# Two transformer layers on one core: where gathers, first weight loads and one pairing copy stand in the order of work

## The chip, the core and the metric

The kernel runs on one core of a Trainium2 chip. Its time is device time in microseconds (us) for one execution. Before the change four runs gave 1397.26 to 1401.92 us, with a median of 1398.56. The engines are named as in the profile: PE is TensorE (matmuls; PEld is its weight load), DVE is VectorE, ACT is ScalarE, POOL is GpSimd. SP only issues DMAs. ACT and POOL issue DMAs too, POOL's being the gathers, whose row numbers come from a tile of indices.

## What is computed

The input x has 64 batches of 32 tokens of 256 numbers. Two layers are added to it, each an attention and a feed-forward part, and each with parameters that a batch picks by an index (`itok_*`). Cut to its core, in float32:

```python
x = x + attn0(einsum('bct,bcd->bdt', x, weights[itok_198]), ...)   # 16 heads of 128, 64 slots a head
x = x + ffn0(cond2(x, Wg, Wu, Wd, Ag, Bg, Au, Bu, Ad, Bd, itok_7)) # low-rank ways per batch
x = x + attn1(cond1(x, W, A, Bm, scalings, itok_6), ...)           # low-rank way per batch
x = x + ffn1(cond3(x, W, b, itok_15), w_gate_up, w_down)           # one of 16 matrices per batch

# in attn0
q, k = rope(hs @ Wq.T), rope(hs @ Wk.T)
s  = clip(hs @ Ws1.T @ Ws2.T + bs2)
ok = exp(-cumlogsumexp(s)) * (tril(q k^T) @ exp(s))
# in cond2, with A = Ag[itok], and so on
gate = x @ Wg + (x @ A) @ B
h = silu(gate) * up
y = h @ Wd + (h @ Ad[itok]) @ Bd[itok]
```

`ffn0` rounds its weights to three values, `ffn1` rounds weights and activations to 8-bit steps.

## The kernel before

The order of instructions is written by hand: each engine runs its own instructions in the order in which the program emits them, and waits for what they read and for the memory that they overwrite.

**Start.** SP loads indices, two tiles of x, wqp (the first 512 columns of Wq), the four strips of ws2 (17 rows each, line 727), more of x, and then the other weights. ACT's queue loads the constants and ws1c. wqp and wkp hold the columns as given; ACT copies them into the order that the rotation wants (L720, two copies each, into wq and wk). The loop over (wq, wk) requests one and copies it before it comes to the next, and wkp is requested by ACT itself (L717). Meanwhile POOL gathers 16 tiles cwt (L744), DVE spreads them into own (L756), TensorE makes hs of the first half group (L766), ACT copies it to hsT (L774), TensorE makes the low rank r (L783) and ACT moves it to rT (L787). Weight tiles of this part come from ten slots; a load into a slot waits until its last tile has been read.

**Phase one, turns -1 to 33.** Each turn works on several of 32 steps (a group of 4 heads by a quarter of two x tiles). For step n+1 it runs slots_exp (L892 reads ws2 and rT, four matmuls, the fourth reading the fourth strip), project_qk (L820; DVE multiplies, L831 and L832; POOL adds, L834 and L835) and cumsum; for step n scores (L940), attend, weigh (POOL makes qe, L987), project_v (L850), project_g (L867) and turn_qe (TensorE reads qe, L1006); for n-1 mix, values, gate and norm (POOL's power, L1077); for n-2 leave (L1100, added to x by DVE, L1106). The generator tabulate() is advanced once after each turn from the third. It writes tables for the later gathers into DRAM: alin and blin; then, for each of eight chunks in one advance, the own tables own_in and own_out by nine gathers into two staged tiles and three stores on SP; then alora and blora. The generator chunk_0() runs the first chunk's first half of phase two inside turns 31 to 33.

**Between the phases** the program emits fetch_down(0), a gather; fetch_linear(0), two loads on SP; lw; and the loads of the attention's weights wqk, sixteen small DMAs (L1231) of which ACT issues eight and SP eight.

**Phase two, turns 0 to 7 of turn2, then drain.** Each turn works on one chunk of 256 tokens: gate_up (L519) with its ways (gate_up_adapters: L534, Silu on ACT L541, product on DVE L542), pair_down (ACT copies the gathered ways of Ad from the tiles ag into adp, L547), down_adapters (TensorE reads adp, L560; DVE writes ud, L566), down (L576, L581; it reads cdt), ffn_up (L600, L604, L605), ffn_down (L619, L624), linear_adapters (L633) and linear (L651). Between them stand attention and scores of chunk n-1 and the experts and 8-bit layers of chunk n-2 (run_experts L1431, quant_up L1461, quant_h, turn_h L1485, quant_down L1501). The gathers for later use are fetch_in (8, into ag), fetch_out (4, into bx), fetch_down (1) and fetch (8 expert matrices `we` and 2 biases `eb`). In gather() a `held` gather first has DVE copy its column of indices into a small tile (L443, sixteen tiles in turn), so that POOL's gather (L445) cannot come before DVE has reached that place; one that is not held reads the index table directly.

Of the kernel before, what the change touches and what calls it, by code (L numbers as in the profile page):

```python
# [15 lines left out]
P = 128  # L16
B = 64
T = 32
D = 256
# [59 lines left out]
def mk_kernel(  # L79
# [250 lines left out]
    own_in = dram.tile([8 * P, D], F32, tag="own_in", name="own_in")  # L330
    own_out = dram.tile([8 * P, D], F32, tag="own_out", name="own_out")

    def tabulate():
        def ways_in(table, src, lo, rows):
            to = table.rearrange("(a p) v -> p a v", p=P)
            with nc.allow_non_contiguous_dma(reason="ranks of an adapter"):
                nc.sync.dma_start(
                    out=to[:, :, lo : lo + 16], in_=src[rows, :].rearrange("p (a i) -> p a i", i=16)
                )

        def every_other(k):
            return slice(k, D, 2)

        for k in range(2):
            ways_in(alin, laT, k * 16, every_other(k))
        yield

        def staged():
            return first.tile([P, D], F32, tag="sg", name="staged", bufs=2)

        t = staged()
        nc.sync.dma_start(out=t, in_=lb)
        nc.vector.tensor_scalar(t, t, scal, None, MULT)
        nc.sync.dma_start(out=blin, in_=t)
        yield
        for ch in range(8):
            rows = slice(ch * P, (ch + 1) * P)
            t = staged()
            for b in range(8):
                at = ch * 8 + b  # L360
                gather(t[:, b * 32 : (b + 1) * 32], alin, idx("lora2", it)[:, at : at + 1], False)
            for k in range(2):
                nc.sync.dma_start(
                    out=own_in[rows, :].rearrange("p (j k b i) -> p k j b i", j=4, k=2, b=2)[:, k],
                    in_=t.rearrange("p (j b k i) -> p k j b i", j=4, k=2, b=2)[:, k],
                )
            t = staged()
            gather(t, blin, lidx[:, ch : ch + 1], False)
            nc.sync.dma_start(out=own_out[rows, :], in_=t)
            yield  # L370
        for i, src in enumerate((ag, au)):
            for k in range(2):
                ways_in(alora, src, k * 32 + i * 16, every_other(k))
            yield
        for k in range(8):
            ways_in(alora, ad, 64 + k * 16, slice(k * P, (k + 1) * P))
            if k % 2:
                yield
        for half in range(2):
            for i, src in enumerate((bg, bu)):  # L380
                rows = slice((2 * half + i) * P, (2 * half + i + 1) * P)
                nc.sync.dma_start(
                    out=blora[rows, :].rearrange("p (k f) -> p k f", k=4),
                    in_=src.rearrange("p (k half f) -> p half k f", k=4, half=2)[:, half, :, :],
                )
                yield
# [283 lines left out]
    with ExitStack() as s1:  # L670
# [41 lines left out]
        ws1c = p1.tile([P, 2, 16], F32, tag="ws1c", name="ws1c")  # L712
        nc.scalar.dma_start(out=ws1c, in_=ws1T.rearrange("(c p) r -> p c r", p=P))

        for name, src, queue in (("wq", wqT, nc.sync), ("wk", wkT, nc.scalar)):
            t, to = slot(f"{name}p", [P, 2, 512]), slot(name, [P, 2, 512])
            queue.dma_start(out=t, in_=src[:, :512].rearrange("(c p) f -> p c f", p=P))  # L717
            weights.setdefault(0, []).append(to)
            for c in range(2):
                nc.scalar.copy(  # L720
                    to[:, c, :].rearrange("p (half h r) -> p half h r", half=2, h=4),
                    t[:, c, :].rearrange("p (h half r) -> p half h r", h=4, half=2),
                )

        ws2 = p1.tile([P, 1024], F32, tag="ws2", name="ws2")
        for i in range(4):
            nc.sync.dma_start(out=ws2[32 * i : 32 * i + 17, :], in_=ws2T)
# [4 lines left out]
        nc.sync.dma_start(out=gnwt, in_=gnw)  # L732
        load_weights(0, ("wo",))
        nc.sync.dma_start(out=scal, in_=lscal)
        load_weights(1)
        ws1 = p1.tile([P, 2, 4, 32], F32, tag="ws1", name="ws1")
        nc.vector.memset(ws1, 0.0)

# [57 lines left out]
        own_weights(1, 2)  # L796
        condition(0, (0,))
        low_rank(0, (0,))
        own_weights(2, 4)

        cosb = const("cos").unsqueeze(1).to_broadcast([P, 16, T])
# [310 lines left out]
        def turn(n):  # L1112

            def on(i, f, *a):
                if 0 <= i < len(steps):
                    f(i, *a)

            def more(*at):

                if n in at:  # L1120
                    next(beyond)

            def ahead():
                if 2 <= n < len(steps):
                    next(preparing, None)

            N = len(steps)
            on(n + 1, slots_exp)
            on(n, scores)
            more(N)  # L1130
            on(n - 1, mix)
            on(n + 1, slots_clip)
            more(N - 1)
            on(n - 2, leave)
            more(N - 1)
            on(n + 1, project_qk, "q", 0)
            on(n + 1, project_qk, "k", 0)
            if n == -1:
                condition(0, (1,))
                own_weights(4, 8)  # L1140
            if n < 2:
                condition(n + 2)
            on(n - 1, values)
            on(n, attend)
            on(n + 1, cumsum)
            more(N)
            on(n, weigh)
            on(n + 1, project_qk, "q", 1)
            on(n + 1, project_qk, "k", 1)
            on(n - 1, gate)  # L1150
            on(n, project_v)
            on(n, project_g)
            if n == -1:
                low_rank(0, (1,))
                own_weights(8, 16)
            if n < 2:
                low_rank(n + 2)
            if n == 1:
                small_tables()
                next(preparing)  # L1160
            ahead()
            more(N - 1)
            on(n, turn_qe)
            ahead()
            on(n - 1, norm)
            more(N)
# [16 lines left out]
            yield  # L1183

        beyond = chunk_0()
        tabulating = tabulate()
        for n in range(-1, len(steps) + 2):
            turn(n)
            if n in (25, 30, 31, 33):
# [26 lines left out]
    bdt = w.tile([P, D], F32, tag="bdt", name="bdt")  # L1216
    fetch_down(0, False)
    adp = w.tile([P, 4, 8, 2, 16], F32, tag="adp", name="adp")
    fetch_linear(0)
    ud = w.tile([P, 2, 4, T], F32, tag="ud", name="ud")  # L1220
    lw = load_w("lw", [P, 2, D], lwT.rearrange("(p c) f -> p c f", c=2))
# [182 lines left out]

    experts = {}

    def fetch(ch, b):


        got = experts.setdefault(ch, {})  # L1410
# [5 lines left out]
        else:  # L1416
# [1 line left out]
            if b == 8:  # L1418
                got[8] = work.tile([P, 2, D], F32, tag="eb", name="eb", bufs=1)
            to = got[8][:, b - 8, :]  # L1420
        gather(to, table, at, True)

    def run_experts(ch, groups=(0, 1)):
        c = chunks[ch]
# [89 lines left out]
    def turn2(n):  # L1514
# [20 lines left out]
        for k in range(8):  # L1535
            gu(k)
            if k == 3:
                if not begun:
                    on(n, gate_up_adapters, 0)
                on(n - 2, run_experts)  # L1540
                for i in range(4):
                    on(n - 1, attn_scores, i)
            elif k == 5:
                on(n - 1, attn_exp)
                on(n, pair_down)
            elif k == 6:
                on(n - 2, turn_y)
        if not begun:
# [2 lines left out]
        if n == 1:  # L1551
            project_values(0)
            tokens_in(2)
        on(n - 1, fetch, 0)
        on(n - 1, fetch, 1)
        on(n - 2, quant_up, 0)
        on(n - 2, quant_h, 0)
        on(n - 1, fetch, 2)
        on(n - 1, fetch, 3)
        on(n, down_adapters)  # L1560
        on(n + 1, fetch_in, 0)
        if not last:
            on(n - 2, quant_up, 1)
            on(n - 2, quant_h, 1)
        for b in range(1, 4):
            on(n + 1, fetch_in, b)
        on(n, down)
        on(n - 2, tokens_back)
        if n != 1:
            on(n + 1, tokens_in)  # L1570
        on(n + 1, fetch_in, 4)
        on(n - 1, fetch, 4)
        if not last:
            on(n - 2, turn_h, 0)
            on(n - 2, turn_h, 1)
        on(n - 1, attn_values)
        on(n, ffn_up, 0)
        on(n + 1, fetch_in, 5)
        on(n - 1, fetch, 5)
        on(n, ffn_up, 1)  # L1580
        on(n + 1, fetch_in, 6)
        on(n - 1, fetch, 6)
        on(n, ffn_up, 2)
        on(n + 1, fetch_in, 7)
        on(n - 1, fetch, 7)
        on(n, ffn_up, 3)
        on(n + 1, fetch_out, 0)
        on(n, ffn_up, 4)
        on(n + 1, fetch_out, 1)
        if last:  # L1590
            on(n - 1, attn_out)
        on(n, ffn_up, 5)
        on(n + 1, fetch_out, 2)
        on(n - 1, fetch, 8)
        on(n - 1, fetch, 9)
        if last:
            on(n - 2, quant_up, 1)
            on(n - 2, quant_h, 1)
            on(n - 1, run_experts)
            for b in range(8):  # L1600
                fetch(7, b)
        else:
            on(n - 2, quant_down, 0)
        on(n + 1, fetch_out, 3)
        on(n, ffn_down)
        if last:
            on(n - 2, turn_h, 0)
# [2 lines left out]
            on(n - 2, quant_down, 1)  # L1610
            on(n - 1, attn_out)
        on(n, linear_adapters)
        on(n + 1, fetch_down)
        on(n, linear)
        on(n + 1, fetch_linear)

    def drain():

        turn_y(6)
        queries_keys(7)  # L1620
        for b in range(8, 10):
            fetch(7, b)
        quant_up(6, 0)
        for k in range(4):
# [2 lines left out]
        project_values(7)  # L1627
        quant_down(5, 0)
        attn_weights(7)
        quant_up(6, 1)  # L1630
        attn_values(7, 2)
        quant_down(5, 1)
# [107 lines left out]
```

## Time and profile before

| | |
|---|---|
| median of the runs | 1398.56 us |
| the profiled execution | 1399.07 us, its span 1397.3 us |
| granted TensorE clock, mean | 0.999 |
| DVE, ACT, POOL busy | 65%, 36%, 39% |
| DMA | 70.27 MB, mean 50 GB/s |
| gathers `we`, mean of one on POOL | 948 ns, x64 |
| copy wk<-wkp on ACT | 1.14 us for two |
| copy adp<-ag on ACT | 1.14 us for two |
| L820 x8, the first / a later one | 3.62 / 1.99 us |
| a turn of phase one, L867 to L867, from 102.89 to 750.84 us | 22.96 to 23.84 us |

The profile is of one execution. Its page gives the busy time of each engine over the span; views of the trace give what an engine waited for (releaser, total, times, longest), the instructions in order of time (start, length, engine, line, tile written<-read), the DMAs issued in a stretch with the median time to landing, and the busy time in stretches.

### The profile page before, as it was taken

What the parts mean: (1) busy time and instruction counts of PE and PEld (TensorE: products, weight loads), DVE (VectorE), ACT (ScalarE), POOL (GpSimd) and SP (SyncE); (2) the same over time, 40 slices, a digit from 0 to 9 for tenths busy, and PEclk for the clock granted to TensorE, in tenths of its full rate; (3) what the DMA queues carried; (4) which work ended last, traced back from release to release, by engine and by line L of the source; (5) the groups of instructions that cost most, each with busy time, mean ns of one, the idle gap of its engine ahead of it and who ended that gap; (6) DMA issues with size and microseconds to landing.
All of it is one profiled execution on the core that took longest, in us unless ns stands there. A gap on an engine that the chain in (4) does not pass through costs nothing.

```text
span 1397.3 us, 37990 instructions
## 1 busy us (share of the span) xinstructions
PE 1363.9 (98%) x16332; PEld 1093.6 (78%) x16332; DVE 913.8 (65%) x1907; ACT 507.6 (36%) x1365; POOL 538.2 (39%) x601
## 2 busy tenths in 40 slices
PE   4999999999999999999999999999999999999997
PEld 3777777777777778777777788888787878888775
DVE  2687888887888888877777425463646364554665
ACT  2454545454545454545454213130312221222221
POOL 5332477777434333333444131423231405050220
PEclk9999999999999999999999999999999999999999
DMA  6120001311312000100001251312131304031220
GB/s 194 50 69 2 5 19 30 95 37 27 63 40 58 10 6 12 42 2 2 13 15 49 60 103 37 98 53 88 44 98 32 110 11 123 10 109 33 69 77 16
DMA packets 96864, 70.27 MB, mean 50 GB/s; under 512 B 66420, under 2 KB 83956, under 8 KB 96696
## 3 DMA queue, kind: packets, MB, share of 16 engines
q0 software_dynamic: 14848, 36.98, 9.2%
q1 hardware_dynamic: 73736, 25.37, 7.5%
q10 hardware_dynamic: 8112, 5.49, 1.4%
q8 instruction: 128, 2.10, 0.6%
q14 instruction: 40, 0.33, 0.1%
HBM read 63.49 MB, written 6.29 MB: 50 GB/s over the span
## 4 chain that ended last, share of the span: by engine, by line
PE 96%; DVE 1%; DMA 1%; ACT 1%; issue 1%; POOL 0%; ACTq 0%; SPq 0%; DVEq 0%
PE ps L820 16%; PE ps L1100 8%; PE ps L519 8%; PE ps L867 8%; PE ps L850 8%; PE ps L1461 6%; PE ps L600 5%; PE ps L576 4%; PE ps L1501 3%; PE ps L619 3%; PE ps L940 3%; PE ps L1049 2%; PE ps L534 2%; PE ps L1267 2%; PE ps L892 1%; PE ps L1067 1%
## 5 line engine op out<-in xcount | busy, mean ns | idle before, releaser
L445 POOL DMA_INDIRECT we<-in_ew,at x64 | 60.7, 948 | 287.0 <-DVE h L1468 213.5
L1106 DVE SCALAR_TENSOR_TENSOR x<-ps,f,x 128x256 f32<-128x256 f32 x256 | 120.7, 482 | 11.9 <-PE ps L1100 0.7
L820 PE MATMUL ps<-hsT,wq 128*128 128x256 f32 x512 | 126.2, 390 | 0.0
L820 PE MATMUL ps<-hsT,wk 128*128 128x256 f32 x512 | 120.9, 379 | 0.0
L1100 PE MATMUL ps<-wo,og 128*128 128x256 f32 x512 | 119.0, 385 | 1.3
L867 PEld LDWEIGHTS ps<-hsT,wg 128*128 128x128 f32 x512 | 97.3, 190 | 26.9 <-issue 15.1
L867 PE MATMUL ps<-hsT,wg 128*128 128x256 f32 x512 | 115.7, 379 | 0.0
L850 PE MATMUL ps<-wv,hsT 128*128 128x512 f32 x256 | 115.2, 593 | 0.0
L1056 ACT ACTIVATE sq<-ps 128x512 f32<-128x512 f32 x64 | 34.8, 595 | 213.0 <-PE ps L1049 213.0
L834 POOL TENSOR_TENSOR qT<-ra,rb 128x256 f32<-128x256 f32 x64 | 46.8, 731 | 168.8 <-DVE rb L832 168.7
L820 PEld LDWEIGHTS ps<-hsT,wq 128*128 128x128 f32 x512 | 95.5, 192 | 18.2 <-issue 4.8
L924 DVE RECIPROCAL enz<-ps 128x256 f32<-128x256 f32 x64 | 107.5, 1721 | 2.8 <-PE ps L915 2.8
L1100 PEld LDWEIGHTS ps<-wo,og 128*128 128x128 f32 x512 | 94.6, 190 | 17.0 <-DVE aT L947 5.2
L820 PEld LDWEIGHTS ps<-hsT,wk 128*128 128x128 f32 x512 | 97.4, 190 | 13.3
L1077 POOL TENSOR_TENSOR f<-f,mhalf 128x8 f32<-128x8 f32 x32 | 54.4, 1701 | 137.5 <-DVE f L1075 137.5
L978 ACT ACTIVATE qv<-ok,nmx 128x64 f32<-128x64 f32 x256 | 85.3, 334 | 30.8 <-DVE nmx L974 29.8
L831 DVE TENSOR_TENSOR ra<-ps,ct 128x512 f32<-128x512 f32 x128 | 85.9, 671 | 3.7 <-PE ps L820 2.0
L832 DVE TENSOR_TENSOR rb<-ps,ct 128x512 f32<-128x512 f32 x128 | 87.0, 680 | 0.0
L850 PEld LDWEIGHTS ps<-wv,hsT 128*128 128x128 f32 x256 | 48.6, 190 | 47.6 <-issue 45.9
L1461 PE MATMUL ps<-guT,y3T 128*128 128x352 f32 x256 | 79.8, 465 | 0.5 <-ACT y3T L407 0.5
L542 DVE TENSOR_TENSOR hT<-ps,sg 128x256 f32<-128x256 f32 x64 | 24.2, 420 | 83.8 <-ACT sg L541 83.8
L445 POOL DMA_INDIRECT ag<-alora,at x56 | 53.0, 947 | 55.6 <-DVE at L443 33.7
(235 smaller groups left out, 2818.0 us busy)
## 6 DMA issues: line engine op xcount, KB each, us to landing
x<-in_x SPq DMA_DIRECT2D x8, 256.0 KB, 16.5
wv<-in_wvT SPq DMA_DIRECT2D x4, 512.0 KB
wg<-in_wgT SPq DMA_DIRECT2D x4, 512.0 KB, 4.2
wo<-in_woT SPq DMA_DIRECT2D x4, 512.0 KB
wq<-in_wqT SPq DMA_DIRECT2D x12, 128.0 KB, 3.0
wk<-in_wkT SPq DMA_DIRECT2D x12, 128.0 KB, 4.2
row<-in_wgu ACTq DMA_DIRECT2D x11, 128.0 KB, 2.2
out<-res SPq DMA_DIRECT2D x5, 256.0 KB, 2.3
```

The lines of the kernel that those rows point to most:

```text
L445: nc.gpsimd.indirect_dma_start(out=to, out_offset=None, in_=table, in_offset=bass.IndirectOffsetOnAxis(ap=at, axis=0))
L519: nc.tensor.matmul(ps[:, i * 256 : (i + 1) * 256], lhsT=mlp[name, k // 4][:, j, part], rhs=c["xT"][:, j, :], start=(i == 0 and j == 0), st ...
L820: nc.tensor.matmul(ps[:, half * 256 : (half + 1) * 256], lhsT=wt[:, c, half * 256 + pr * P : half * 256 + (pr + 1) * P], rhs=hs[:, c, lo : ...
L831: nc.vector.tensor_tensor(by_t(a.rearrange("p h t -> p (h t)")), by_t(ps), cosb, MULT)
L832: nc.vector.tensor_tensor(by_t(b.rearrange("p h t -> p (h t)")), by_t(ps), sinb, MULT)
L850: nc.tensor.matmul(ps, lhsT=hs[:, c, lo + gi * P : lo + (gi + 1) * P], rhs=w[2][:, c, :], start=(c == 0), stop=(c == 1),)
L867: nc.tensor.matmul(ps[:, e * 256 : (e + 1) * 256], lhsT=w[3][:, c, h * P : (h + 1) * P], rhs=hs[:, c, lo : lo + 256], start=(c == 0), stop ...
L924: nc.vector.reciprocal(t[:, e, :], banks[e][:, :256])
L978: nc.scalar.activation(qv[:, k, :], ok[:, k, :], AF.Exp, bias=nmx[:, k : k + 1], accum_out=rs[:, k : k + 1],)
L1100: nc.tensor.matmul(ps[:, e * D : (e + 1) * D], lhsT=s["og"][:, h, gi * P : (gi + 1) * P], rhs=w[4][:, h, :], start=True, stop=True,)
L1106: nc.vector.scalar_tensor_tensor(xq[q][:, gi, :], ps[:, e * D : (e + 1) * D], s["f2"][:, of : of + 1], xq[q][:, gi, :], MULT, ADD,)
L1461: nc.tensor.matmul(ps[:, :352], lhsT=c["y3T"][:, k, gi * P : (gi + 1) * P], rhs=guT[:, k, lo : lo + 352], start=(k == 0), stop=(k == 1),)
```

## The change

1. wqp and wkp are both requested before any copy. The copy of wq comes where it was; the copy of wk, and the load of the second group of weights, come after the first low_rank.
2. The own tables leave tabulate() for a generator of their own, advanced inside turns from the fifth, just ahead of weigh, three gathers at a time.
3. pair_down(0) is emitted right after adp exists, ahead of fetch_linear(0) and of wqk's loads, and no longer in turn 0 of phase two.
4. In phase two, four of fetch and three of fetch_in (all eight in turn 0) follow attn_exp; the other five fetch_in follow down_adapters; four fetch follow attn_values; fetch_out, the biases and fetch_down follow ffn_up 0 to 3. For the last chunk four expert gathers are not held, and the other six come in the drain in two places.

```diff
+    def own_tables():
+        for ch in range(8):
+            rows = slice(ch * P, (ch + 1) * P)
+            t = staged()
+            for b in range(8):
+                at = ch * 8 + b
+                gather(t[:, b * 32 : (b + 1) * 32], alin, idx("lora2", it)[:, at : at + 1], False)
+                if b % 3 == 2:
+                    yield
+            for k in range(2):
+                nc.sync.dma_start(
...
+            t = staged()
+            gather(t, blin, lidx[:, ch : ch + 1], False)
+            nc.sync.dma_start(out=own_out[rows, :], in_=t)
+            yield
...
+        as_given = []
         for name, src, queue in (("wq", wqT, nc.sync), ("wk", wkT, nc.scalar)):
-            t, to = slot(f"{name}p", [P, 2, 512]), slot(name, [P, 2, 512])
-            queue.dma_start(out=t, in_=src[:, :512].rearrange("(c p) f -> p c f", p=P))
-            weights.setdefault(0, []).append(to)
+            as_given.append(slot(f"{name}p", [P, 2, 512]))
+            queue.dma_start(out=as_given[-1], in_=src[:, :512].rearrange("(c p) f -> p c f", p=P))
+
+        def in_order(which):
+            to = slot("w" + "qk"[which], [P, 2, 512])
+            weights.setdefault(0, []).insert(which, to)
             for c in range(2):
                 nc.scalar.copy(
...
+        in_order(0)
...
-        load_weights(1)
...
         low_rank(0, (0,))
+        in_order(1)
+        load_weights(1)
         own_weights(2, 4)
...
             more(N)
+            if n >= 5:
+                next(owning, None)
             on(n, weigh)
...
     adp = w.tile([P, 4, 8, 2, 16], F32, tag="adp", name="adp")
+    pair_down(0)
     fetch_linear(0)
...
             elif k == 5:
                 on(n - 1, attn_exp)
-                on(n, pair_down)
+                if not begun:
+                    on(n, pair_down)
+                for b in range(4):
+                    on(n - 1, fetch, b)
+                for b in range(8 if begun else 3):
+                    on(n + 1, fetch_in, b)
...
         on(n, down_adapters)
-        on(n + 1, fetch_in, 0)
+        if not begun:
+            for b in range(3, 8):
+                on(n + 1, fetch_in, b)
...
         on(n - 1, attn_values)
+        for b in range(4, 8):
+            on(n - 1, fetch, b)
         on(n, ffn_up, 0)
-        on(n + 1, fetch_in, 5)
-        on(n - 1, fetch, 5)
+        for j in range(2):
+            on(n + 1, fetch_out, j)
         on(n, ffn_up, 1)
...
-            for b in range(8):
-                fetch(7, b)
+            for b in range(4):
+                fetch(7, b, False)
...
         queries_keys(7)
-        for b in range(8, 10):
+        for b in (4, 5, 8):
             fetch(7, b)
...
         attn_weights(7)
+        for b in (6, 7, 9):
+            fetch(7, b)
         quant_up(6, 1)
```

More of the change, by code (lines that the diff above doesn't have):

```diff
@@ L331, in mk_kernel, with staged @@
     own_out = dram.tile([8 * P, D], F32, tag="own_out", name="own_out")
+    def staged():
+        return first.tile([P, D], F32, tag="sg", name="staged", bufs=2)
+    def own_tables():
[9 more added lines that the diff above has]
+                nc.sync.dma_start(
+                    out=own_in[rows, :].rearrange("p (j k b i) -> p k j b i", j=4, k=2, b=2)[:, k],
+                    in_=t.rearrange("p (j b k i) -> p k j b i", j=4, k=2, b=2)[:, k],
+                )
+            t = staged()
+            gather(t, blin, lidx[:, ch : ch + 1], False)
+            nc.sync.dma_start(out=own_out[rows, :], in_=t)
+            yield
     def tabulate():
@@ L346, in tabulate @@
         yield
-        def staged():
-            return first.tile([P, D], F32, tag="sg", name="staged", bufs=2)
         t = staged()
@@ L355, in tabulate @@
         yield
-        for ch in range(8):
-            rows = slice(ch * P, (ch + 1) * P)
-            t = staged()
-            for b in range(8):
[L360 to L370, printed above, removed]
         for i, src in enumerate((ag, au)):
@@ L721, in mk_kernel @@
                     to[:, c, :].rearrange("p (half h r) -> p half h r", half=2, h=4),
-                    t[:, c, :].rearrange("p (h half r) -> p half h r", h=4, half=2),
+                    as_given[which][:, c, :].rearrange("p (h half r) -> p half h r", h=4, half=2),
                 )
+        in_order(0)
         ws2 = p1.tile([P, 1024], F32, tag="ws2", name="ws2")
@@ L1185, in mk_kernel @@
         beyond = chunk_0()
-        tabulating = tabulate()
+        tabulating, owning = tabulate(), own_tables()
         for n in range(-1, len(steps) + 2):
@@ L1405, in mk_kernel, with fetch @@
     experts = {}
-    def fetch(ch, b):
+    def fetch(ch, b, held=True):
         got = experts.setdefault(ch, {})
@@ L1420, in fetch @@
             to = got[8][:, b - 8, :]
-        gather(to, table, at, True)
+        gather(to, table, at, held)
     def run_experts(ch, groups=(0, 1)):
@@ L1553, in turn2 @@
             tokens_in(2)
-        on(n - 1, fetch, 0)
-        on(n - 1, fetch, 1)
         on(n - 2, quant_up, 0)
         on(n - 2, quant_h, 0)
-        on(n - 1, fetch, 2)
-        on(n - 1, fetch, 3)
         on(n, down_adapters)
-        on(n + 1, fetch_in, 0)
+        if not begun:
+            for b in range(3, 8):
+                on(n + 1, fetch_in, b)
         if not last:
@@ L1564, in turn2 @@
             on(n - 2, quant_h, 1)
-        for b in range(1, 4):
-            on(n + 1, fetch_in, b)
         on(n, down)
@@ L1570, in turn2 @@
             on(n + 1, tokens_in)
-        on(n + 1, fetch_in, 4)
-        on(n - 1, fetch, 4)
         if not last:
@@ L1576, in turn2 @@
         on(n - 1, attn_values)
+        for b in range(4, 8):
+            on(n - 1, fetch, b)
         on(n, ffn_up, 0)
-        on(n + 1, fetch_in, 5)
-        on(n - 1, fetch, 5)
+        for j in range(2):
+            on(n + 1, fetch_out, j)
         on(n, ffn_up, 1)
-        on(n + 1, fetch_in, 6)
-        on(n - 1, fetch, 6)
+        for j in range(2, 4):
+            on(n + 1, fetch_out, j)
         on(n, ffn_up, 2)
-        on(n + 1, fetch_in, 7)
-        on(n - 1, fetch, 7)
+        on(n - 1, fetch, 8)
+        on(n - 1, fetch, 9)
         on(n, ffn_up, 3)
-        on(n + 1, fetch_out, 0)
+        on(n + 1, fetch_down)
         on(n, ffn_up, 4)
-        on(n + 1, fetch_out, 1)
         if last:
@@ L1592, in turn2 @@
         on(n, ffn_up, 5)
-        on(n + 1, fetch_out, 2)
-        on(n - 1, fetch, 8)
-        on(n - 1, fetch, 9)
         if last:
@@ L1599, in turn2 @@
             on(n - 1, run_experts)
-            for b in range(8):
-                fetch(7, b)
+            for b in range(4):
+                fetch(7, b, False)
         else:
             on(n - 2, quant_down, 0)
-        on(n + 1, fetch_out, 3)
         on(n, ffn_down)
@@ L1612, in turn2 @@
         on(n, linear_adapters)
-        on(n + 1, fetch_down)
         on(n, linear)
```

## The prediction, made before the changed kernel ran

> **What bounds the kernel now.** I read the head of the page first, then the table of what TensorE waited for, then the instructions in time around its longest waits, and last what SP's queue waited for.
>
> ```profile
> span 1397.3 us, 37990 instructions
> ...
> PE 1363.9 (98%) x16332; PEld 1093.6 (78%) x16332; DVE 913.8 (65%) x1907; ACT 507.6 (36%) x1365; POOL 538.2 (39%) x601
> ```
>
> TensorE is busy for 1363.9 of 1397.3 us, so a change that removes no matmul can win 33.4 us at most, and only where TensorE stands still. The table of its waits (line, releaser: total us, times, longest) says where:
>
> ```profile
> PE ps L766 <- DVE own L756: 10.1, 2, 9.9
> PE ps L783 <- ACT hsT L774: 6.0, 1, 6.0
> PE ps L1485 <- DVE h L216: 3.8, 2, 2.5
> PE ps L560 <- ACT adp L547: 3.2, 1, 3.2
> ```
>
> The first two lie in the first 20 us, the third in the last 40, the fourth is one stall at 799 us. Asked stretch by stretch, the table has 0.4 us of waits between 45 and 760 us, and between 760 and 1320 us 3.2 (adp), 0.8, 0.2 and 0.2. The stretches in which most gathers are moved therefore have nothing to give.
>
> The start, in order of time (start, us, engine, line):
>
> ```profile
> 7.74 0.46 ACTq L717 DMA_DIRECT2D wkp<-in_wkT  x1
> ...
> 11.34 1.22 PE L766 MATMUL ps<-own,x 128*128 128x128 f32 x4 [0.26 <-DVE own L756]
> ...
> 17.07 1.14 ACT L720 COPY wk<-wkp 128x512 f32<-128x512 f32 x2 [8.20 <-DMA wkp<-in_wkT]
> ...
> 18.11 0.64 ACT L774 COPY hsT<-ps 128x256 f32<-128x256 f32 x2
> ...
> 20.64 0.47 ACT L787 ACTIVATE rT<-ps,ct 128x256 f32<-128x256 f32 x1 [1.89 <-PE ps L783]
> ...
> 22.34 3.62 PE L820 MATMUL ps<-hsT,wq 128*128 128x256 f32 x8
> ```
>
> ACT requests wkp only behind the copies of wq, then stands 8.20 us in front of the copy of wk, and hsT, which TensorE has had ready since 12.56, is copied behind it. That is the 6.0 us wait. But what SP's queue waits for, and what the DMAs issued at 4 to 6 us took, show a second limit at the same place:
>
> ```profile
> SPq L685 <- DMA ws<-in_ws2T: 3.6, 1, 3.6
> SPq L118 <- DMA ws<-in_ws2T: 2.3, 1, 2.3
> ...
> x<-in_x SPq DMA_DIRECT2D x2, 256.0 KB, 16.9
> ```
>
> The four strips of ws2 (68 KB each, requested from 2.67 to 4.37) are still landing when SP issues wg (17.94, after waiting 3.6) and the last x (about 21.07, after 2.3). Estimate: two landings 3.1 us apart are 68 KB at 22 GB/s, while from 2 to 4 us the queues moved 289 GB/s; and x tiles requested behind the strips took 16.9 us. The strips trickle in one after the other, the last at about 21.07. Slots_exp's fourth matmul (L892) reads it.
>
> Third place, at 796 us:
>
> ```profile
> 796.47 4.43 ACTq L1231 DMA_DIRECT2D wqk<-in_wqkv  x8
> ...
> 801.08 1.14 ACT L547 COPY adp<-ag 128x512 f32<-128x512 f32 x2 [4.25 <-DMA wqk<-in_wqkv]
> ...
> 802.27 1.10 PE L560 MATMUL ps<-hT,adp 128*32 128x64 f32 x64 [3.24 <-ACT adp L547]
> ```
>
> ACT issues eight DMAs for 4.43 us before the two copies for which TensorE stands.
>
> **Part 1, first weights.** wkp goes to ACT's queue behind ct and ws1c, near 1.65. It then shares the DMA engines with x0, x1 and wqp, which landed at 7.72 (in the chain of waits 2.16 + 5.56): 512 KB at the 287 GB/s of 4 to 6 us is 1.8 us, so wqp lands at 9.5 at worst and wq's two copies (0.61 each) end at 10.8, before L766 ends (12.56). The copy of hsT starts at 12.6 instead of 18.11. From it rT ended 3.0 later (18.11 to 21.11), so rT is there at 15.6, 5.5 early. wk's copies (1.14) follow rT, to 16.8; wk is first read 3.15 after wq.
>
> Then L892: its fourth matmul waits for the last strip. The DMA work queued ahead of that strip is the same bytes in another order (wkp landed at 17.04, 7.74 + 9.30 in the chain, ahead of it before too), so it lands at 21.07 again, 0.1 before L892 started in the old order (21.17). Only the three earlier matmuls come out of the way: L892 to L820 took 1.17, of which I take about half, 0.64. L820's first eight matmuls ran slowly (3.62 against 1.99 later) until 25.49, with the page's clock column at full all the time. If that moment stays, 0.64 of slow work is 0.64 x 1.99/3.62 = **0.35 us**. Bounds: 5.5 if the strip doesn't hold it; below zero, because TensorE now idles from about 15.1 to 21.1. If the slow stretch lasted as long from 21.1 as it did from 18.53 (6.96), it would end 2.57 later, which costs 2.57 x (1 - 0.55) = 1.2 less 0.35, a loss of 0.8.
>
> [...]
>
> Covered: POOL's cond gathers and two memsets end at 23.86 and delay qT only if L820 comes before about 21; after it POOL idles 6 us (30.87 to 36.95). The second weights stay behind the same requests on SP; the slots they take are wqp's and wkp's, free by 17.
>
> **Part 2, adp.** The copies go ahead of wqk's DMAs: ACT's Silu ends at 796.83, plus 1.14 is 797.97. L1100 ends at 799.02 and L560 follows: 802.27 - 799.05 = **3.2 us**. Next late: L576's second half reads the cdt tile requested at 799.1. L576 would start at 800.1 and reach it 16 matmuls (half of 7.17) later, at 803.7. The same load (cut, issued 766.60) had moved its bytes by 769.9, 3.3 us on; so about 802.5, plus some contention with wqk's DMAs, which now start 1.1 later. As no wait was seen at 806.9, the bounds are 3.2 and 0. I take 3.2, since 3.3 is the nearest row. What is behind those eight DMAs on ACT is yT's copy at 811; wqk is read at 831.
>
> **Part 3, own tables.** The same 72 gathers, 9 in each of 8 turns before, 3 in each of 24 turns now, ahead of weigh's qe on POOL. One takes 1.25 us with its gap. In the turn before the first gathers POOL ended kT at 165.84 and began qe at 168.89, when qv came; three gathers last to 169.6, so qe is 0.8 late, and TensorE reads it at 175.0. Before, qe came 3 us late (239.13) and TensorE did not wait. **0.** Without that cover each late us would cost 24. SP's 24 stores wait for them as before.
>
> **Part 4, phase two.** Per turn the same 23 gathers. Seven index copies (about 0.5 us) move behind attn_scores, where VectorE idles 4.60 us (1288.48 to 1293.08, nothing run). Their tiles were freed by run_experts and by pair_down just before. Four copies (0.3) now stand ahead of gT's products; ACT's third Silu (1243.96) waits for the first of these, which ended at 1243.54 and would end at 1243.9. All landings come earlier or stay; in the drain the expert gathers 6, 7 and 9 go out at about 1355.7 to 1359.2 and land 3.3 later, at 1361.5, against their use at 1364.7 (weights) and 1367.4 (bias). **0**, bounds plus and minus 1. Eight copies (0.57) leave the way to xT at 1331.19, where L633 waited: **0.2**.
>
> **Sum.** 0.35 + 3.2 + 0.2 = 3.75 us. The profiled execution, 1399.07 with a span of 1397.3, becomes 1395.3; it stood 0.5 above the median of 1398.56, which becomes **1394.8**. About 0.3% (4.2 us, 1394.4) is what a measurement can tell from no change, so this is "within" by a hair.
>
> **Rivals.** *The start comes forward whole* (the strips do not hold): 5.5 + 3.2 + 0.2 = 8.9, 1389.7. For it: the 6.0 us wait names ACT. Against: 21.07. Chance 0.07. *cdt takes adp's place:* the wait moves from L560 into L576, 3.2 is lost, 1398.0. For it: wqk's DMAs slide onto cdt's; against: 3.3 us of landing with 4.6 available. Chance 0.10. *Slower: POOL before qe.* If POOL spent more than (175.0 - 1.5 - 165.84)/3 = 2.6 us on each own gather, by waiting for its staged tile or its landing, TensorE would stall in 24 turns; at the 3.3 us in which gathers land, 2.2 x 24 = 53, 1448. Against: gathers follow each other in 1.25, and the two staged tiles are stored turns before they are reused. Chance 0.09. *The moves do nothing:* that is the forecast's zero for Parts 3 and 4.
>
> **Numbers.** Forecast 0.74, with its own range 1392.8 to 1396.8; 0.4 of it (0.30) falls beyond 1394.4. Faster: 0.30 + 0.07 = 0.37. Within: 0.44 + 0.10 = 0.54. Slower 0.09. Range 1391.0 to 1398.4.
>
> **To look for.** Right: L560's wait gone; L892's last matmul near 21 with rT long done, L820 at 21.5 to 22; ACT's copies of wk behind rT. Wrong: L820 before 19; a wait inside L576; waits at L1006, or a turn over 23.2 us from the fifth on; L1431 waiting in the drain.

## The result, and the profile after

| | before | changed |
|---|---|---|
| median | 1400.16 us (54 runs, 1396.52 to 1402.94) | 1395.41 us (33 runs, 1393.20 to 1398.79) |
| the profiled execution, its span | 1399.07, 1397.3 | 1397.05, 1395.3 |

The ratio is 0.9965, with a 95% interval from 0.9960 to 0.9971: 4.75 us between the medians. The two profiled executions lie only 2.0 us apart: that of before is among the shorter of its runs, that of the changed kernel among the longer. Where their heads differ, the repeated experiments decide, not these two.

These runs were taken where the kernel before takes about 1400 us, and so was the first set of experiments, on one chip. The other sets fell on two other chips, where the same kernel takes 1511 to 1514 us. Those give another answer for the moved gathers; they come second. The ratios that stand with intervals below are not plain ratios of two medians, and can differ a little from them.

The table of what TensorE waited for, changed kernel (line, releaser: us in total, times, longest):

```profile
PE ps L776 <- DVE own L766: 11.2, 1, 11.2
PE ps L904 <- DMA ws<-in_ws2T: 4.6, 2, 3.1
PE ps L1500 <- DVE h L216: 3.8, 2, 2.5
```

The wait for hsT (6.0) and the wait for adp (3.2) are gone. New is the second line: L904 is slots_exp, and it waits for the strips of ws2. The start in order of time (start, us, engine, line, tile, idle before it):

```profile
1.66 0.52 ACTq L724 DMA_DIRECT2D wkp<-in_wkT  x1
...
12.93 0.80 ACT L784 COPY hsT<-ps 128x256 f32<-128x256 f32 x2 [0.69 <-PE ps L776]
15.46 0.47 ACT L797 ACTIVATE rT<-ps,ct 128x256 f32<-128x256 f32 x1 [1.74 <-PE ps L793]
...
19.98 1.22 PE L904 MATMUL ps<-rT,ws 17*128 17x256 f32 x2 [3.10 <-DMA ws<-in_ws2T]
22.67 1.22 PE L904 MATMUL ps<-rT,ws 17*128 17x256 f32 x2 [1.48 <-DMA ws<-in_ws2T]
23.82 3.78 PE L832 MATMUL ps<-hsT,wq 128*128 128x256 f32 x8
27.39 2.67 PE L832 MATMUL ps<-hsT,wk 128*128 128x256 f32 x8
```

hsT and rT are there 5.2 us sooner than before, and TensorE then stands in front of the third and the fourth strip. The wait has moved from ACT to a DMA.

The place between the phases, changed kernel:

```profile
798.68 0.61 ACT L553 COPY adp<-ag 128x512 f32<-128x512 f32 x1
...
800.91 1.10 PE L566 MATMUL ps<-hT,adp 128*32 128x64 f32 x64
...
801.94 7.28 PE L582 MATMUL ps<-hT,cdt 128*128 128x256 f32 x32
...
805.49 3.32 PEld L582 LDWEIGHTS ps<-hT,cdt 128*128 128x128 f32 x16 [0.24 <-DMA cdt<-in_cd]
```

In the program the copies of adp come ahead of wqk's DMAs now, and L566 follows L1112 (the L1100 of before) without a wait. The load of cdt arrives a moment late: the second half of L582's weight loads waits 0.24 for it, and L582 takes 7.28 where it took 7.17.

### The profile page after: what moved, and what is told of

Its sections match the earlier page's. It is cut to its first block, busy times and chain, and to the rows that moved or that the text cites. A ratio compares the mean times of both kernels' runs of the same rounds, so it can differ in the third digit from the quotient of the medians.

```text
span 1395.3 us, 37984 instructions
## 1 busy us (share of the span) xinstructions
PE 1365.4 (98%) x16332; PEld 1094.3 (78%) x16332; DVE 911.1 (65%) x1903; ACT 507.7 (36%) x1365; POOL 541.1 (39%) x601
## 4 chain that ended last, share of the span: by engine, by line
PE 96%; DMA 2%; DVE 2%; issue 0%; ACT 0%; POOL 0%; SPq 0%; DVEq 0%
PE ps L832 17%; PE ps L1112 8%; PE ps L525 8%; PE ps L879 8%; PE ps L862 8%; PE ps L1476 6%; PE ps L606 5%; PE ps L582 4%; PE ps L1516 3%; PE ps L625 3%; PE ps L952 3%; PE ps L1061 3%; PE ps L540 2%; PE ps L1282 2%; PE ps L904 1%; DMA ws<-in_ws2T 1%
## 5 line engine op out<-in xcount | busy, mean ns | idle before, releaser
L451 POOL DMA_INDIRECT we<-in_ew,at x60 | 56.8, 946 | 318.5 <-DVE at L449 178.4
L832 PE MATMUL ps<-hsT,wq 128*128 128x256 f32 x512 | 126.4, 390 | 0.0
L832 PE MATMUL ps<-hsT,wk 128*128 128x256 f32 x512 | 121.7, 381 | 0.0
L1112 PE MATMUL ps<-wo,og 128*128 128x256 f32 x512 | 119.0, 385 | 1.3
L832 PEld LDWEIGHTS ps<-hsT,wq 128*128 128x128 f32 x512 | 95.5, 192 | 18.2 <-issue 6.2
L832 PEld LDWEIGHTS ps<-hsT,wk 128*128 128x128 f32 x512 | 98.0, 191 | 13.5
L1112 PEld LDWEIGHTS ps<-wo,og 128*128 128x128 f32 x512 | 94.7, 190 | 17.0 <-DVE aT L959 5.2
L451 POOL DMA_INDIRECT ag<-alora,at x56 | 56.6, 1011 | 49.8 <-DVE at L449 29.8
```

The source lines that it names most:

```text
L451: nc.gpsimd.indirect_dma_start(out=to, out_offset=None, in_=table, in_offset=bass.IndirectOffsetOnAxis(ap=at, axis=0))
L832: nc.tensor.matmul(ps[:, half * 256 : (half + 1) * 256], lhsT=wt[:, c, half * 256 + pr * P : half * 256 + (pr + 1) * P], rhs=hs[:, c, lo : ...
L1112: nc.tensor.matmul(ps[:, e * D : (e + 1) * D], lhsT=s["og"][:, h, gi * P : (gi + 1) * P], rhs=w[4][:, h, :], start=True, stop=True,)
```

## Experiments where the kernel before takes 1400 us

Each part was put alone into the kernel before. In this set its median was 1400.44 us over 29 runs.

**One early pair_down.**

```diff
     adp = w.tile([P, 4, 8, 2, 16], F32, tag="adp", name="adp")
+    pair_down(0)
     fetch_linear(0)
...
-                on(n, pair_down)
+                if not begun:
+                    on(n, pair_down)
```

> The kernel before with one edit: pair_down(0) ahead of fetch_linear(0) and wqk. Forecast's Part 2: L560's wait of 3.2 us is gone and nothing takes its place, ratio 0.9977 (3.2 of 1400). If cdt's second half took the place, ratio 0.999 to 1.000 and TensorE waits inside down.

Measured: 1395.72 us (11 runs), ratio 0.9972 (0.9962 to 0.9983), which is 3.9 us with bounds of 2.4 and 5.3 (4.7 between the medians). Its table of waits has no line for adp, and the wait for cdt's second half is 0.34. This part alone gives the gain of the whole change, within the intervals.

**The head alone**: both requests first, wk's copies and the second weights behind low_rank (the diff's in_order and as_given, nothing else).

> The kernel before with Part 1 alone (wkp requested first, its copy after low_rank). Three theories. The forecast: the last strip lands when it did, L820 starts 0.64 earlier, ratio 0.9997. What the changed kernel's profile shows at the start (last strip at 22.6, L820 at 23.8 and slow until 30): 2.4 us lost, ratio 1.0017. The strips don't matter: 5.5 us won, ratio 0.996.

Measured: 1400.36 us (12 runs), ratio 1.0004 (0.9991 to 1.0018). TensorE in order of time:

```profile
17.68 0.98 PE L898 MATMUL ps<-rT,ws 17*128 17x256 f32 x2 [1.39 <-DMA ws<-in_ws2T]
21.07 1.22 PE L898 MATMUL ps<-rT,ws 17*128 17x256 f32 x2 [2.40 <-DMA ws<-in_ws2T]
22.21 3.78 PE L826 MATMUL ps<-hsT,wq 128*128 128x256 f32 x8
25.79 3.09 PE L826 MATMUL ps<-hsT,wk 128*128 128x256 f32 x8
```

The last strip lets its matmul go at 21.07. L826 follows at 22.21, against 22.34 before. The 5 us by which hsT came sooner are all given back here. The same request order let the last strip's matmul go at 22.67 in the changed kernel's profile, at 21.07 here, and at 21.25 in a second profile of the changed kernel (on a slower chip, below). So 22.67 need not come from the new order.

The median rules out the third theory, that the strips don't matter (0.996). It can't tell the first, a gain of 0.64, from the second, a loss of 2.4: 0.9997 and 1.0017 both lie in the interval. One more row speaks for a loss. The busy time of TensorE between 18 and 28 us (stretch, length, busy us and count, granted clock, DMA share, GB/s), first before, then with the head alone:

```profile
18.00:28.00 10.00, 8.90 (x33) 1.00 0.72 203
```

```profile
18.00:28.00 10.00, 7.60 (x18) 0.50 0.71 206
```

While TensorE stands in front of the strips, its granted clock falls to 0.50, and it is back at 1.00 only after 28 us. The second L826 starts 1.2 later than before (33.45 against 32.26).

**The gathers alone** (Parts 3 and 4, the own tables and phase two):

> The kernel before with Parts 3 and 4 alone: own tables inside the turns, gathers of phase two moved. Forecast: 0.2 us won, ratio 0.9999. The two traces lie 0.8 us further apart at turn 7 of phase two than at turn 0: if the moved gathers did that, ratio 0.9994. POOL in front of qe: above 1.0.

Measured: 1400.11 us (12 runs), ratio 0.9999 (0.9987 to 1.0011). Nothing, on this chip. Its one profile has a loss at one place, between the phases:

```profile
802.16 1.94 PE L566 MATMUL ps<-hT,adp 128*32 128x64 f32 x64 [3.21 <-ACT adp L553]
804.03 9.05 PE L582 MATMUL ps<-hT,cdt 128*128 128x256 f32 x32
```

The two took 1.10 and 7.17 before, 2.7 us less, and take 1.10 and 7.28 in the whole change. The experiments on the slower chips show why.

**The changed kernel with the strips cut.** Each strip has 17 rows. Here 16 rows go in one DMA, and the last row in another that is cut into 16 pieces:

```diff
         for i in range(4):
-            nc.sync.dma_start(out=ws2[32 * i : 32 * i + 17, :], in_=ws2T)
+            nc.sync.dma_start(out=ws2[32 * i : 32 * i + 16, :], in_=ws2T[:16, :])
+        for i in range(4):
+            nc.sync.dma_start(
+                out=ws2[32 * i + 16 : 32 * i + 17, :].rearrange("o (a b) -> o a b", a=16),
+                in_=ws2T[16:17, :].rearrange("o (a b) -> o a b", a=16),
+            )
```

> The changed kernel, with each strip of ws2 loaded as 16 rows and one row instead of 17 rows. If the strips trickle because 17 rows go one way, they land before 10 us, L904's waits for ws are gone, and the first long product (L832) starts near 17 instead of 23.8: about 5 us won against the changed kernel, more if TensorE no longer slows; ratio to the kernel before 0.992 to 0.993. If the strips are slow for another reason, as the changed kernel: 0.9965.

Measured: 1386.43 us (5 runs), ratio 0.9907 (0.9891 to 0.9923), more than had been expected and the fastest version of this study. TensorE in order of time:

```profile
12.52 2.07 PE L781 MATMUL ps<-own,x 128*128 128x128 f32 x8 [12.52 <-DVE own L771]
14.63 2.08 PE L798 MATMUL ps<-hsT,ws 128*128 128x256 f32 x4
17.27 0.87 PE L909 MATMUL ps<-ws,rT 17*128 17x256 f32 x2 [0.56 <-ACT rT L802]
...
18.06 0.75 PE L909 MATMUL ps<-rT,ws 17*128 17x256 f32 x2
18.74 3.78 PE L837 MATMUL ps<-hsT,wq 128*128 128x256 f32 x8
```

No matmul of L909 waits for a strip, and L837 starts at 18.74, which is 5.1 sooner than in the changed kernel's profile and 3.6 sooner than before. So the strips were the limit that stood behind ACT's copies, and they were slow as DMAs of 17 rows: the last one, requested at 4.19 in the changed kernel's profile, let its matmul go at 22.67, 18.5 us later, while the DMAs of 16 rows here land after a median of 9.7 us. Over how many DMA engines a strip went, no view shows. Of the 9.0 us between the medians the profiles show 5.3 (spans 1395.3 and 1390.0), and 5.1 of these in the head. The profiled run took 1391.79 us and the other four 1386.18 to 1386.86, so the rest lies in runs that were not profiled, and where it comes from is not shown.

## Experiments where the kernel before takes 1511 to 1514 us

The next experiments were meant to divide the gain of the cut strips. They fell on slower chips, and showed something else first. The kernel before was not profiled there; where a profile with its gathers is needed, that of the kernel with the strips cut alone stands in.

**Cut strips alone, and with the early pair_down** (two kernels, the same edits as above in the kernel before; the second was run in both sets):

> The kernel before, with only the four strips of ws2 loaded as sixteen rows and one row cut in sixteen pieces. Theory (the change's new request order is what brings hsT forward; without it wk's copies still hold it): the strips land early but L892 waits for rT at about 20.6 as before, L820 starts near 22, time 1400.0 within 1.2. Rival (the slow strips also delayed wk itself and the x tiles requested behind them): wk lands 3 us or more earlier, L820 near 19, time 1395 to 1397.

> The kernel before, with the same cut of the strips and pair_down(0) early, and nothing else of the change. Theory (the new request order pays once the strips are fast): 1395.5 if the strips alone bring nothing, and in any case 4 us or more above the 1386.4 of the changed kernel with cut strips. Rival (the strips did it all, the request order nothing): 1386 to 1387.5.

> The kernel before with cut strips and pair_down(0) early, once more. Where before takes about 1400: theory (the strips bring the 2.9 us by which L825 started earlier in the profile of the strips alone, and pair_down 4.4) 1392 to 1393.5, so that the new request order is worth 5 to 6 us of the 1386.4 of the changed kernel with cut strips; rival (the strips did it all) 1386 to 1387.5. Where before takes 1511: 1510 within 2, as in the second batch.

Measured, against 1511.41 (23 runs): 1513.68, ratio 1.0011 (1.0000 to 1.0022), and 1510.59, ratio 0.9991 (0.9980 to 1.0002). The second again, against 1513.99 (15 runs): 1511.35, ratio 0.9981 (0.9972 to 0.9990). The first two expectations were written for a chip of 1400 us; the third had 1510 within 2 for this one, and held. The kernel with the strips cut alone shows where a part of the 110 us more goes. Its waits of TensorE:

```profile
PE ps L1054 <- issue: 34.2, 44, 1.8
PE ps L1378 <- issue: 13.3, 26, 1.5
```

"Issue" is time in which the engine waited for nothing that the profile shows. L1054 (before: L1049) is the stream of sixty-four 64x64 matmuls in gate's norm. One such stream, from the same kernel's timeline:

```profile
278.22 1.89 PE L825 MATMUL ps<-hsT,wq 128*128 128x256 f32 x8
...
281.77 0.81 PE L1054 MATMUL ps<-w2T,v 64*64 64x64 f32 x38
...
283.38 0.95 POOL L445 DMA_INDIRECT staged<-alin,it  x1 [0.30 <-issue]
...
285.63 0.35 PE L1054 MATMUL ps<-w2T,v 64*64 64x64 f32 x4 [1.10 <-issue]
...
287.07 0.49 PE L1054 MATMUL ps<-w2T,v 64*64 64x64 f32 x3 [1.09 <-issue]
...
288.55 0.62 PE L1054 MATMUL ps<-w2T,v 64*64 64x64 f32 x11 [0.99 <-issue]
```

The profile of the kernel before, from the chip where it takes 1400, at the same place in its turn, with the same gathers beside it:

```profile
255.03 1.16 PE L1049 MATMUL ps<-w2T,v 64*64 64x64 f32 x64
...
255.38 0.96 POOL L445 DMA_INDIRECT staged<-alin,it  x1 [0.30 <-DVE rb L832]
```

Sixty-four matmuls take 1.16 us there, and over 7 us (281.77 to 289.27) here, broken by waits, while nine gathers run from 275.51 to 286.86. The eight longer matmuls of L825 ahead of them, beside the same gathers, take 1.89 us and lose nothing in issue.

**The changed kernel, and its gathers alone, on such a chip.** No edit: the changed kernel itself, and the kernel before with Parts 3 and 4.

> The changed kernel itself, once more. On a chip where the kernel before takes about 1400: 1395.4 within 1. On a chip like that of the second batch (before 1511): if the gathers moved beside long products are what spares TensorE its waits for issue there, 1440 to 1455; if the head or the sixteen early matmuls were, about 1507.

> The kernel before with Parts 3 and 4 alone, once more. Where before takes about 1400: 1400 within 1, as in the first batch. Where it takes 1511: theory (a stream of small matmuls waits for its issue while gathers run beside it, so that moving the gathers takes the waits away) 1445 to 1460, with hardly any wait for issue on TensorE before 760; rival (the waits come from elsewhere) 1511 within 3.

Measured, against 1513.99: the changed kernel 1439.60 us, ratio **0.9507** (0.9494 to 0.9520); the gathers alone 1450.71, ratio 0.9575 (0.9558 to 0.9592). The changed kernel, which gives 0.35% on one chip, gives 5% on another, and the gathers, which give nothing on the one, are most of it on the other. The changed kernel's stream on this chip, where the three gathers come behind it:

```profile
301.60 1.16 PE L1061 MATMUL ps<-w2T,v 64*64 64x64 f32 x64
...
304.85 1.07 POOL L451 DMA_INDIRECT staged<-alin,it  x1 [0.16 <-issue]
```

The busy time of a stretch, first for the kernel with the strips cut alone, then for the changed kernel on the slower chip (stretch, its length, busy us of PE, PEld, DVE, ACT and POOL with counts, granted clock of TensorE, DMA share, GB/s):

```profile
220.00:310.00 90.00, 77.15 (x870) 59.43 (x863) 55.21 (x95) 32.91 (x96) 49.64 (x56) 0.89 0.20 48
```

```profile
220.00:310.00 90.00, 89.81 (x1196) 70.06 (x1195) 76.90 (x131) 42.96 (x127) 44.97 (x52) 1.00 0.25 52
```

The column before the last two shows the second half of the cost: where TensorE stalls, its granted clock is lower, 0.89 in this stretch. Within the stream shown it is 1.00 until 285 us and 0.50 from 286 to 292, and the eight products of wq behind it take 2.84 us (from 290.91) where the eight ahead of it take 1.89.

The first gate_up (L519, L525 in the changed kernel) marks the end of phase one. It starts at 835.54 with the gathers as before and the strips cut, at 833.7 and 832.3 in the two profiles with the early pair_down too, and at 770.40 with Parts 3 and 4 alone: 65.1 us between the first and the last of these. On the chip of 1400 us it starts at 770.29 in the kernel before. So Part 3, the only part that moves gathers of phase one, takes away the whole loss of that phase. The waits at L1054 are 34.2 of the 65.1. The lower clock is about 27 by an estimate (90 us stretches from 130 to 490 us granted 0.96, 0.89, 0.89 and 0.96: 90 x 0.30), which counts some us twice, since TensorE also waits while the clock is low. A count over one turn agrees: from the start of the stream to the second products of wk behind it 11.81 us pass here and 3.87 in the kernel before (281.77 to 293.58, 255.03 to 258.90), and eight such turns would be 63.5.

Phase two, from that start to the end of the span, took 676.4 us in the kernel with the strips cut alone, 676.5 and 676.1 with the early pair_down too, 680.1 with Parts 3 and 4, and 667.1 in the changed kernel. On the chip of 1400 us it takes 627.0 before and 623.1 in the changed kernel, so here the change leaves most of the loss of phase two in place. Part 4 moves waits rather than takes them away: with the gathers as before, L1378 (attn_values) waits 13.3 for issue and L560 (down_adapters) not at all; in the changed kernel the same line of attn_values waits 3.9, and L566 (the L560 of before) 13.1.

The gathers alone do worst, and the place between the phases shows it. First the gathers alone, then the changed kernel:

```profile
802.26 0.94 POOL L451 DMA_INDIRECT ag<-alora,at  x1 [5.04 <-ACT adp L553]
802.35 1.70 PE L566 MATMUL ps<-hT,adp 128*32 128x64 f32 x50 [3.21 <-ACT adp L553]
...
809.40 2.64 PE L582 MATMUL ps<-hT,cdt 128*128 128x256 f32 x5 [1.02 <-issue]
...
821.50 1.03 PE L587 MATMUL ps<-ud,bdt 128*128 128x256 f32 x4
```

```profile
799.36 1.10 PE L566 MATMUL ps<-hT,adp 128*32 128x64 f32 x64
...
802.55 0.94 POOL L451 DMA_INDIRECT ag<-alora,at  x1 [5.04 <-issue]
...
807.72 1.03 PE L587 MATMUL ps<-ud,bdt 128*128 128x256 f32 x4
```

Part 4 puts eight gathers into ag here. With the late pair_down they are released by the same copies of adp as L566, and run beside it: 19.15 us from L566 to L587. With the early pair_down L566 is done when they start: 8.36. These 10.8 us and the wait of 3.2 for adp cover the 13.0 between the two phases, and the medians lie 11.1 apart. So on such chips Part 4 needs Part 2. The early pair_down alone is 3.1 between the medians (1513.68 and 1510.59), about the size that it has on the other chip.

**The changed kernel with cut strips and the old request order** (Parts 2, 3 and 4 with the cut, without Part 1):

> The changed kernel with cut strips, but with the request order of the head as before (Parts 2, 3 and 4 and the cut, without Part 1). Where the kernel before takes about 1400: theory (the new request order pays 5 to 6 us once the strips are fast) 1392 to 1393.5; rival (the cut of the strips did all of it) 1386 to 1387.5. Where before takes 1511 to 1514: theory (the gathers of Part 3 are what counts there, and the head nothing that can be seen) 0.947 to 0.953 of before, the first L525 at 769 to 772 us as in the changed kernel's second profile, not at 835; rival (Part 1 has a share there) 0.957 or more.

Measured, against 1513.40 (8 runs): 1440.14 us, ratio 0.9511 (0.9494 to 0.9529), first L525 at 771.67, both as expected of the theory that only the gathers count. So Part 1 has no share in the 5%. Nor is it needed in the head. In the four profiles with cut strips and the old order the first products of wq start at 19.46, 19.91, 18.61 and 19.05, against 18.74 with the new order. The kernel with the strips cut alone shows why (ACT):

```profile
9.15 0.37 ACTq L717 DMA_DIRECT2D wkp<-in_wkT  x1
...
13.89 1.14 ACT L720 COPY wk<-wkp 128x512 f32<-128x512 f32 x2 [3.61 <-DMA wkp<-in_wkT]
```

wkp lands within 4.7 us of its request. In the kernel before it took 9.3. It is not the chip: on one and the same slower chip ACT's copy of wk starts 8.7 us after the request in the gathers alone, with strips of 17 rows (7.52 to 16.25), and 4.6 after it with cut strips and the early pair_down (8.42 to 13.02). The strips of 17 rows had held up the very load for which ACT waited. Cutting them takes away both waits of the head at once. Whether the old order with cut strips also reaches 1386 where before takes 1400 was not measured: no such run fell on such a chip.

**Sixteen matmuls of constants ahead of the first product**, in the changed kernel with cut strips, run in both sets:

```diff
+        warm = bank()
+        for _ in range(16):
+            nc.tensor.matmul(warm[:, :256], lhsT=const("ident"), rhs=ct[:, :256], start=True, stop=True)
         own_weights(0, 1)
```

> The changed kernel with cut strips, and sixteen matmuls of constants on TensorE ahead of the first product, while it waits for the first gathered tables (their result is read by nobody). Theory (the array runs at half rate for some microseconds after it begins, and the head's first products pay for it: 3.78 and 2.7 us for two groups of eight that take 1.99 and 1.89 later): those groups start at the later rate, 3 to 4 us less, 1382.5 to 1383.5. Rival (the slow stretch is set by something else, such as the loads running beside it): 1386.4 within 0.8. If the sixteen end after the tables are there (about 12.5 us), up to 1 us more than 1386.4.

> The changed kernel with cut strips and sixteen early matmuls, once more. Where before takes about 1400: theory (the array's first microseconds at half rate are paid in the head) 1382.5 to 1383.5; rival (the slow stretch has another cause) 1386.4 within 0.8. Where before takes 1511: 1443 within 3, as in the second batch.

Measured: 1443.25 us, ratio 0.9543 (0.9527 to 0.9559), and 1448.21, ratio 0.9561 (0.9548 to 0.9574); slower than the changed kernel by 0.4 to 0.5% of before. The second expectation, 1443 within 3, was missed by 2 us. Behind them the first product of L781 ran at the later rate, its eight matmuls in 1.05 us (2.07 without them). But ACT then stood 13.9 us in the one profile and 13.7 in the other before it copied hsT, TensorE stood 13.0 us for it in both, and after that stand the rate was low again (3.78 for the first eight of L840). No view names what ACT waited for. The question of what a fast head is worth stays open.

## Why the prediction held, and where its reasons did not

**Where before takes 1400, the forecast of 1394.8 stands 0.6 from the median of 1395.41.** Against the larger sample of before (1400.16) the gain is 4.75 where 3.75 had been summed.

**Part 2 was right in place and size.** The wait in front of adp was predicted at 3.2 us and measured, alone, at 3.9 (2.4 to 5.3). What was named as late next, cdt, took 4.5 us to land (requested at 801.0, there at 805.5) and not the 3.3 of "the nearest row". It costs about 0.1, so it did not take adp's place, but it had little to spare.

**Part 1 was right that the strips, not ACT, hold L892; its term of 0.35 was not confirmed.** The last strip came at 21.07 in the run of the head alone, as predicted. The term measured -0.6, with bounds of +1.3 and -2.5. "L820 at 21.5 to 22" was 22.21 alone and 23.82 in the changed kernel. One step was off: wqp "lands at 9.5 at worst" took until 11.1. L776's first product starts only at 11.24 itself, so the copy of hsT came at 12.93 instead of 12.6.

The term rested on "if that moment stays", the end of the slow stretch at 25.49. It did not stay. With the head alone the granted clock is 0.50 until about 28.2, close to the 28.06 of the prediction's other case, in which the slow stretch lasts as long from 21.1; in the changed kernel's profile it is 0.50 until about 29. The second L832 starts 2.4 later there than before (34.64 against 32.26), and 1.2 later with the head alone, where that case had a loss of 0.8. So the profiles follow the bound and not the term. The medians can't tell the two apart, and that the sum came out so near is in part luck: Part 2 gave more than its 3.2 by the middle of its interval, and Part 1 less than its 0.35.

The rival that the whole head comes forward (1389.7) fell by the strips; with the strips cut the head did come forward.

**Parts 3 and 4 at zero were right where before takes 1400** (0.9999, 0.9987 to 1.0011), and POOL did not delay qe: no wait at its readers. The prediction took Parts 2 and 4 one by one. That Part 4's gathers meet L566 unless Part 2 lets it go first, 2.7 us in the one profile of the gathers alone, was not seen.

**Elsewhere one step failed: "The stretches in which most gathers are moved therefore have nothing to give."** It was read from the table of waits of one execution on one chip, where the stretch from 45 to 760 us has 0.4 us of waits. On the slower chips the kernel with the gathers as before loses 65 us in phase one, and Part 3 takes all of it away. The trace from which the forecast was made could not show this price. It did show what it hangs on: a stream of sixty-four short matmuls beside a burst of nine gathers.

## What to carry to other kernels

A wait that ends last may hide another right behind it: ACT's copy and the strips both stood in front of the same products, so bringing one forward gave nothing until the other was cut. Before moving requests about, look for a load whose landing time doesn't fit its bytes; here 17 rows cut into 16 and 1 brought more than the whole change (9.0 us between the medians against 4.75).

Keep gathers away from streams of short matmuls even where a profile shows no wait there (one stream took 1.16 us beside gathers on the one chip and over 7 on a slower one), and try such a move on more than one chip: its worth went from nothing to over 4%. Part 3 both spreads the gathers, three at a time, and takes them from beside the stream; which of the two counts was not tried apart. Look as well at what a gather is moved next to: Part 4 put some beside another such stream, L566.

## What the runs showed of the hardware that was not expected

**Chips differ in more than a constant factor.** The same kernel took 1400 us on one chip and 1511 to 1514 on two others. In phase one the extra time stood in waits for issue of short matmuls (64x64) beside gathers (34.2 us at L1054), and in the clock that was lower with them (0.89 to 0.96 in the stretches from 130 to 490 us); in phase two a part of it stood in such waits too (13.3 us at L1378 with the gathers as before, 13.1 at L566 in the changed kernel). What differs between the chips is not known. In front of L1054 TensorE stood 34.2 us for issue, and its weight loads 48.9, largely at the same time; in front of the same line in the first profile of before it was nothing and 10.0. No view says what an issue waits for.

**At the start, the profile's clock column did not show the array's rate.** Sixteen matmuls on constants (two records each) began at 3.19 us. The records in each microsecond, for the first of the two runs (stretch, length, busy PE and count, clock, DMA share, GB/s):

```profile
5.00:6.00 1.00, 1.00 (x4) 1.00 0.98 247
...
8.00:9.00 1.00, 1.00 (x5) 1.00 0.87 158
9.00:10.00 1.00, 1.00 (x7) 1.00 0.44 79
...
11.00:12.00 1.00, 1.00 (x7) 1.00 0.16 45
```

About four matmul records a microsecond until about 8.5, then seven, with the clock column at 1.00 throughout. So the rate nearly doubled some 5 us after TensorE began. After 13 us of standing still it was low again, and this time the column shows it:

```profile
20.00:30.00 10.00, 2.54 (x8) 0.50 1.12 258
```

The head of the kernel before is the first case: its first eight of L820 take 3.62 us against 1.99 later, with the column at 1.00.
